# Scores of a query block in two neighbouring banks, and narrow exponentials shared by heads, in an attention and expert-layer kernel

## The chip, the core and the metric

The kernel runs on one core of one Trainium2 chip. The metric is the device time of one execution in microseconds, as the median of several executions. A core has a matrix engine (TensorE, PE in the profile; PEld is its weight load), a vector engine (VectorE, DVE), a scalar engine (ScalarE, ACT), GpSimd (POOL) and SyncE (SP), which issues DMAs. Each takes its instructions in order. Matrix products are written to PSUM, which has 8 banks of 512 float32 columns on 128 partitions; ACT and DVE read them from there.

## The reference

The input x has 4 batches of 1024 tokens with 256 features. The first layer is causal attention with 16 heads of 16 features, whose queries, keys and values go through a latent of 64; half of each head's features are turned by rotary embeddings. The second layer has 8 experts, of which each token takes 2, chosen by a router with three Sinkhorn rounds.

```python
q = concat([q_c, rope(q_e)]); k = concat([k_c, rope(k_e)])
att = softmax(where(causal, q @ k.T / sqrt(16), -inf))
x = layernorm(x + (att @ v) @ Wc)
gates = sinkhorn((x @ router_w.T + router_b) / temperature, 3)
w, idx = top_k(gates, 2)
out = sum(w_j * ((relu(x @ wg[idx_j]) * (x @ wp[idx_j])) @ wo[idx_j]))
x = layernorm(x + (x + out))
```

## The kernel before

The program is written as one stream of instructions, and the framework orders each engine's queue by priority (program order, which some parts move forward) and by a planned time line; it also gives out the buffers of each pool and adds the waits. So a tile of a pool can be taken when an earlier one of that pool has been read for the last time.

**PSUM.** Eight banks, in four pools: `ps_mx` (3 banks), `ps_st` (2), `ps_bg` (2) and `ps_ac` (1, sums of attention times values). `any_tile` hands out banks of the first three in turn, for the start and the end, where no attention needs them.

**Attention** goes over units: a batch and a group of 4 heads, with queries in two halves of 512 (in the last batch the halves are units of their own). It makes the scores twice.

- `row_max` (L342) makes them as queries by keys, 128 queries at a time, in `mx` tiles of one bank (L354, L355). For the first half of the queries there is one score tile of 128 to 512 keys, for the second half a full one of 512 and then one of 128 to 512. A full tile off the diagonal is reduced by `tensor_reduce` (L361), one on the diagonal by an instruction that adds the causal mask and takes the maximum (L364). L370 merges the two maxima. The 16 columns of maxima of 4 heads and 4 query blocks are then transposed (L373, in an `mx` bank), negated and split into two bfloat16 rows by ACT and DVE (L375, L376), and two small DMAs from the ACT queue put them under the queries as rows 96 and 97.
- `attend` (L399) makes them as keys by queries, a key block of 128 at a time, for 4 heads in turn, in `st` tiles of one bank (L433, L434); the two extra rows subtract the maxima. ACT takes the exponential into `pT` (L438), one instruction for each head. On the four diagonal key blocks of a half the columns shrink: 512, 384, 256, 128. POOL sets what lies above the diagonal to zero (L447; in the last two units DVE does, L443). `values` (L412) multiplies by the values (L418) and ACT copies the sum out (L423).

**Side work** is given out in small steps beside attention, and all of it takes its PSUM tiles from `ps_bg`: `project` (queries and keys of a coming batch in four chunks of 128 rows, then values), `finish` (normalize y, output projection, layer norm, logits of the router), and `route` (Sinkhorn, top 2, positions in lists that are scattered to memory by POOL's indirect DMAs). The row maxima get a priority 200 ahead, and may run 44 steps ahead of attention (`LEAD`). The first expert is gathered while the last batch's attention runs. The finish of the last half runs alone, with banks from `any_tile` and `own_tile`.

**Experts** follow: `slot` (L963 on) takes 512 rows of one expert, or 256 for the further ones, makes gate and linear part in `mx` tiles in four chunks, ACT and DVE evacuate them (L977, L978), and the output goes through `st` tiles and is added to memory by indirect DMAs. A last layer norm reads the rows back.

Of the kernel before, what the change touches and what calls it, by code (L numbers as in the profile page):

```python
# [9 lines left out]
F32 = mybir.dt.float32  # L10
# [6 lines left out]
N_MX, N_ST, N_BG = (3,2,2)  # L17
# [10 lines left out]
NMX = 1  # L28
# [7 lines left out]
P = 128  # L36
# [7 lines left out]
def kernel(  # L44
# [60 lines left out]
    def mx_tile(name):  # L105
        return ps_mx.tile([P, QC], F32, tag="mx", name=name)
# [7 lines left out]
    turn = [0]  # L114

    def any_tile(name):

        turn[0] += 1
        return (mx_tile, bg_tile, mx_tile, st_tile, bg_tile, mx_tile, st_tile)[turn[0] % 7](name)
# [30 lines left out]
    for half in range(NQC):  # L150
# [8 lines left out]
    mask = const.tile([P, QC], F32, name="mask")  # L159
    nc.gpsimd.memset(mask, 0.0)  # L160
    nc.gpsimd.affine_select(
        out=mask[:, QC - P :], in_=mask[:, QC - P :], pattern=[[-1, P]], compare_op=ALU.is_ge,
# [72 lines left out]
    def project(b, half, tile_):  # L235
# [40 lines left out]
        pair = []  # L276
        for o in range(2):
            pair.append(chunk(o))
            yield 1.3
        for o in range(2):  # L280
            t1 = proj.tile([P, QC], F32, tag="t1", name=f"t1_{n}_{o}", bufs=R_BUFS)
            nc.vector.tensor_tensor(t1, pair[o], rope[:, 2 * o, cols], ALU.mult)
            t2 = proj.tile([P, QC], F32, tag="t2", name=f"t2_{n}_{o}", bufs=R_BUFS)
            nc.vector.tensor_tensor(t2, pair[1 - o], rope[:, 2 * o + 1, cols], ALU.mult)
            lean.tensor_tensor(t1, t1, t2, ALU.add)
            store(o, t1, lean, [(qk, DHE + o * DHE // 2, DHE // 2) for qk in range(2)])
            yield 0.2
# [54 lines left out]
    def row_max(unit):  # L342

        b, gs, qcs = unit
        for g, half in [(g, qc) for g in gs for qc in qcs]:
            q, k = stack(unit, g)
            n = f"{b}_{g}_{half}"
            mx = work.tile([P, NQC, HG * BPQ], F32, tag="mx", name=f"mx{n}", bufs=2)
            for h in range(HG):
                for t in range(BPQ):  # L350
                    t0 = half * QC + t * P
                    for k0 in range(0, t0 + P, QC):
                        w = min(t0 + P - k0, QC)
                        ps = mx_tile(f"s{n}_{h}_{t}_{k0}")  # L354
                        nc.tensor.matmul(  # L355
                            ps[:, :w], lhsT=q(h, half)[:NROW, t * P : (t + 1) * P], rhs=k(h, k0 // QC)[:NROW, :w],
                            start=True, stop=True,
                        )
                        m = mx[:, k0 // QC, h * BPQ + t : h * BPQ + t + 1]
                        if k0 < half * QC:  # L360
                            nc.vector.tensor_reduce(m, ps, AX.X, ALU.max)  # L361
                        else:
                            dump = work.tile([P, QC], BF16, tag="dump", name=f"d{n}_{h}_{t}", bufs=2)
                            nc.vector.tensor_tensor_reduce(  # L364
                                out=dump[:, :w], in0=ps[:, :w], in1=mask[:, QC - w :],
                                scale=1.0, scalar=MASKED, op0=ALU.add, op1=ALU.max, accum_out=m,
                            )
                        yield
            for j in range(1, half + 1):
                nc.vector.tensor_tensor(mx[:, 0], mx[:, 0], mx[:, j], ALU.max)  # L370
            R = HG * BPQ
            tp = mx_tile(f"mxT{n}")
            nc.tensor.transpose(tp[:R, :P], mx[:, 0], ident)  # L373
# [25 lines left out]
    def attend(unit):  # L399
# [25 lines left out]
        for g, qc in [(g, qc) for g in gs for qc in qcs]:  # L425
            q, k = stack(unit, g)
            for kb in range((qc + 1) * BPQ):
                lo = max(0, kb * P - qc * QC)
                n = f"{b}_{g}_{qc}_{kb}"
                pT = exps.tile([P, HG, QC], F32, tag="pT", name=f"pT{n}")  # L430
                for h in range(HG):
                    late = unit in units[len(units) - NMX :]
                    st = (mx_tile if late and h % 2 else st_tile)(f"sT{n}_{h}")  # L433
                    nc.tensor.matmul(  # L434
                        st[:, lo:], lhsT=k(h, kb // BPQ)[: NROW + 2, kb % BPQ * P : (kb % BPQ + 1) * P],
                        rhs=q(h, qc)[: NROW + 2, lo:], start=True, stop=True,
                    )
                    nc.scalar.activation(pT[:, h, lo:], st[:, lo:], AF.Exp, scale=scale)  # L438
# [875 lines left out]
```

## Time and profile before

| | |
|---|---|
| median of 9 runs | 1121.56 us (1112.28 to 1129.08) |
| profiled execution | 1117.93 us; span of its instructions 1116.2 us |
| mean granted TensorE clock | 0.953 |
| first score matmul of `row_max` / of `attend` | 48.6 us / 67.7 us |
| last score matmul of `attend` | 740.7 us |
| experts' first / last gate matmul | 744.6 us / 1074.9 us |

A profile line of a group reads: line, engine, operation, output and inputs by the program's names, shapes, count, then busy time in all and mean nanoseconds of one, then the engine's idle time just before these and what ended it. A wait line reads: who waited, for whom, total, times and the longest. A timeline line reads: start, length, engine, what, how many in a row, and the idle time before. Matmuls overlap and their ends are modelled, so a busy TensorE need not be at its peak.

### The profile page before, as it was taken

The page shows a single profiled execution, that of the slowest core. Times are in us where ns is not written, and L with a number is a line of the kernel's source. Part 1 is how long each engine was busy: PE and PEld are TensorE (multiplying, and loading weights), DVE is VectorE, ACT ScalarE, POOL GpSimd, SP SyncE. Part 2 cuts the span into 40 slices and gives each one's busy share as a digit, 9 for nine tenths or more (in the row PEclk, how much of TensorE's full clock was granted, in tenths as well). Part 3 has the DMA queues.
Part 4 walks back from the last instruction along what each step waited for, and adds up shares of the span by engine and source line. Part 5 has one row for each costly group of instructions (what it writes and reads, how often), then busy time and mean ns, then how long its engine had stood idle before and what let it go on. Part 6 is the DMA issues. An engine that isn't in the chain of part 4 may idle for free.

```text
span 1116.2 us, 18329 instructions
## 1 busy us (share of the span) xinstructions
PE 987.1 (88%) x6040; PEld 580.7 (52%) x6040; DVE 751.8 (67%) x2300; ACT 643.4 (58%) x1474; POOL 481.8 (43%) x551
## 2 busy tenths in 40 slices
PE   6688999999999998999799799599999799999960
PEld 4444333355434254533244233158888688888860
DVE  4778777888987786887437688147667345646536
ACT  3445666656766564676566576366555355656633
POOL 7167511121635422441423402632566786554544
PEclk9889999999999998999999999699999899999995
DMA  7573420231331330441123220136655356665647
GB/s 261 165 212 111 115 66 15 77 115 40 100 105 29 92 97 19 136 112 49 49 70 114 61 61 3 27 123 188 157 110 147 90 103 161 125 164 101 160 60 301
DMA packets 71367, 119.68 MB, mean 107 GB/s; under 512 B 16416, under 2 KB 43040, under 8 KB 70880
## 3 DMA queue, kind: packets, MB, share of 16 engines
q1 hardware_dynamic: 48544, 81.76, 23.7%
q0 software_dynamic: 20672, 36.41, 15.1%
q8 instruction: 50, 0.82, 0.3%
q10 hardware_dynamic: 2048, 0.27, 0.2%
q14 instruction: 53, 0.43, 0.1%
HBM read 82.52 MB, written 35.60 MB: 106 GB/s over the span
## 4 chain that ended last, share of the span: by engine, by line
PE 72%; ACT 8%; DVE 7%; DMA 5%; issue 5%; SPq 2%; another core or an unknown queue 1%; POOL 1%; ACTq 0%; DVEq 0%; POOLq 0%
PE y L418 14%; PE sT L434 11%; PE s L355 10%; ACT pT L438 4%; PE gp L197 3%; PE gp L198 3%; PE gp L196 3%; PE po L594 3%; PE eo L196 3%; PE eo L198 3%; PE eo L197 3%; PE lp L197 2%; PE lp L198 2%; PE lp L196 2%; DVE mx L361 2%
## 5 line engine op out<-in xcount | busy, mean ns | idle before, releaser
L438 ACT ACTIVATE pT<-sT 128x512 f32<-128x512 f32 (+3 forms) x768 | 347.8, 491 | 210.2 <-PE sT L434 155.9
L364 DVE CUSTOM_DVE_ANT_0 d<-s,mask 128x128 bf16<-128x128 f32 (+3 forms) x512 | 238.0, 483 | 68.1 <-PE s L355 51.7
L434 PE MATMUL sT<-qs,ks 98*128 98x512 bf16 (+3 forms) x768 | 235.2, 334 | 32.8 <-ACT pT L438 16.3
L355 PE MATMUL s<-ks,qs 96*128 96x512 bf16 (+3 forms) x768 | 224.5, 334 | 27.9 <-DMA ks<-parts 7.7
L447 POOL TENSOR_SCALAR_AFFINE_SELECT pT<-pT 128x512 f32<-128x512 f32 x120 | 76.7, 640 | 285.6 <-ACT pT L438 269.3
L361 DVE TENSOR_REDUCE mx<-s 128x1 f32<-128x512 f32 x256 | 175.3, 685 | 31.0 <-PE s L355 28.8
L418 PE MATMUL y<-pT,va 128*32 128x512 f32 (+3 forms) x1536 | 186.1, 512 | 1.1 <-POOL pT L447 0.9
L355 PEld LDWEIGHTS <-qs 96*128 96x128 bf16 x768 | 72.0, 99 | 138.5 <-issue 106.8
L434 PEld LDWEIGHTS <-ks 98*128 98x128 bf16 x768 | 72.5, 99 | 128.7 <-issue 98.0
L995 POOL DMA_INDIRECT results<-eo,ents x64 | 104.8, 1638 | 79.3 <-ACT eo L994 63.3
L196 PE MATMUL eo<-wh,hh 128*128 128x256 f32 x280 | 81.3, 292 | 6.5 <-ACT eo L994 6.4
L190 DVE TENSOR_TENSOR wl<-w,wh 128x512 fp32r<-128x512 f32 x108 | 69.9, 684 | 21.3 <-ACT wh L189 19.9
L921 POOL DMA_INDIRECT xg<-x_rows,ents x64 | 65.3, 1021 | 41.6 <-PE xgT_ps L960 19.7
L978 DVE TENSOR_TENSOR relu<-relu,lp 128x512 f32<-128x512 f32 x64 | 43.8, 684 | 57.2 <-ACT relu L977 23.1
L418 PEld LDWEIGHTS y<-pT,va 128*32 128x32 f32 x1536 | 33.4, 109 | 88.9 <-issue 54.7
L197 PE MATMUL eo<-wl,hh 128*128 128x256 f32 x280 | 79.5, 285 | 0.0
L813 POOL DMA_INDIRECT pairs<-ent,so_i x64 | 65.9, 1030 | 29.5 <-issue 18.1
L198 PE MATMUL eo<-wh,hl 128*128 128x256 f32 x280 | 77.9, 284 | 0.0
L977 ACT ACTIVATE relu<-gp 128x512 f32<-128x512 f32 (+1 forms) x76 | 42.7, 563 | 60.9 <-PE gp L198 40.9
L190 DVE TENSOR_TENSOR hl<-relu,hh 128x512 fp32r<-128x512 f32 (+1 forms) x76 | 48.6, 647 | 28.1 <-ACT hh L189 20.8
L189 ACT CAST wh<-w 128x512 fp32r<-128x512 f32 x108 | 60.5, 619 | 9.5 <-PE gp L197 6.3
L196 PE MATMUL gp<-xh,wh 128*128 128x512 f32 (+1 forms) x176 | 63.6, 368 | 2.2 <-issue 1.1
(209 smaller groups left out, 1795.0 us busy)
## 6 DMA issues: line engine op xcount, KB each, us to landing
ks<-parts SPq DMA_DIRECT2D x90, 128.0 KB
w<-in_wg_dram SPq DMA_DIRECT2D x18, 512.0 KB
w<-in_wp_dram SPq DMA_DIRECT2D x18, 512.0 KB
w<-in_wo_dram SPq DMA_DIRECT2D x18, 512.0 KB
qs<-parts SPq DMA_DIRECT2D x66, 128.0 KB
parts<-lv POOLq DMA_DIRECT2D x12, 384.0 KB
parts<-lv POOLq DMA_DIRECT2D x24, 192.0 KB
xh<-in_x_t_dram SPq DMA_DIRECT2D x8, 512.0 KB
```

The lines of the kernel that those rows point to most:

```text
L190: (sub or nc.vector).tensor_tensor(lo, src, hi.bitcast(F32), ALU.subtract)
L196: nc.tensor.matmul(ps, lhsT=sh, rhs=mh, start=(i == 0), stop=False)
L197: nc.tensor.matmul(ps, lhsT=sh, rhs=ml, start=False, stop=False)
L198: nc.tensor.matmul(ps, lhsT=sl, rhs=mh, start=False, stop=(i == n - 1))
L355: nc.tensor.matmul(ps[:, :w], lhsT=q(h, half)[:NROW, t * P : (t + 1) * P], rhs=k(h, k0 // QC)[:NROW, :w], start=True, stop=True,)
L361: nc.vector.tensor_reduce(m, ps, AX.X, ALU.max)
L364: nc.vector.tensor_tensor_reduce(out=dump[:, :w], in0=ps[:, :w], in1=mask[:, QC - w :], scale=1.0, scalar=MASKED, op0=ALU.add, op1=ALU.max ...
L418: nc.tensor.matmul(acc[g, qc][SLOT * h : SLOT * (h + 1), lo:], lhsT=va[b % 2][:, kb, at : at + SLOT], rhs=pT[:, h, lo:], start=(kb == 0), ...
L434: nc.tensor.matmul(st[:, lo:], lhsT=k(h, kb // BPQ)[: NROW + 2, kb % BPQ * P : (kb % BPQ + 1) * P], rhs=q(h, qc)[: NROW + 2, lo:], start=T ...
L438: nc.scalar.activation(pT[:, h, lo:], st[:, lo:], AF.Exp, scale=scale)
L447: diagonal[0] = nc.gpsimd.affine_select(out=block, in_=block, pattern=[[0, HG], [1, P]], compare_op=ALU.is_ge, fill=0.0, base=0, channel_m ...
L995: ins = nc.gpsimd.indirect_dma_start(out=results[:, :], out_offset=bass.IndirectOffsetOnAxis(ap=k.ent[:, j, 1:2], axis=0), in_=eo, in_offs ...
```

## The change

- An `mx` tile is two neighbouring banks, and there are 2 of them; `bg` has one bank. `st` and `ac` stay at 2 and 1.
- In `row_max`, both score tiles of a query block of the second half lie in one `mx` tile, and one masked instruction over 640 to 1024 columns takes their maximum; L361 and L370 are gone. In the first half, two query blocks share an `mx` tile, a bank each, with an instruction each as before. The mask is bfloat16 and 1024 wide. The transpose of the maxima goes to a `bg` tile.
- In `attend`, two heads share an `st` bank where the columns are 256 and four where they are 128, with one exponential for all of them. In the last unit, where the columns are 384 or 512, the first two heads take a bank each of an `mx` tile and share an exponential.
- In `project`, each of the two chunks with rotary features is multiplied by both tables at once, right behind its matmuls; there are four buffers for the products where there were two.
- In `finish`, the logits take a tile for each two token blocks, which is added to the bias at once, where one tile held four.
- `any_tile` and `own_tile` hand out halves of `mx` tiles; `rows` of the first expert and the last `finish` use `st` tiles; gate and linear part of an expert chunk lie in one `mx` tile.
- `prepare` zeroes rows of the results from a tile of its own, not from the mask.

```diff
-N_MX, N_ST, N_BG = (3,2,2)
+N_MX, N_ST, N_BG = (2,2,1)
     def mx_tile(name):
-        return ps_mx.tile([P, QC], F32, tag="mx", name=name)
+        return ps_mx.tile([P, 2 * QC], F32, tag="mx", name=name)
...
-        return (mx_tile, bg_tile, mx_tile, st_tile, bg_tile, mx_tile, st_tile)[turn[0] % 7](name)
+        if not (turn[0] % 7) % 2:
+            if not spare:
+                both = mx_tile(name)
+                spare.append(both[:, QC:])
+                return both[:, :QC]
+            return spare.pop()
+        return (bg_tile, st_tile, st_tile)[turn[0] % 7 // 2](name)
...
-        pair = []
+        own, others = [], []
         for o in range(2):
-            pair.append(chunk(o))
+            ps = chunk(o)
+            for of, tag, row in ((own, "own", 2 * o), (others, "oth", 3 - 2 * o)):
+                t = proj.tile([P, QC], F32, tag=f"{tag}{o}", name=f"{tag}{n}_{o}", bufs=R_BUFS)
+                nc.vector.tensor_tensor(t, ps, rope[:, row, cols], ALU.mult)
+                of.append(t)
             yield 1.3
         for o in range(2):
...
-            lean.tensor_tensor(t1, t1, t2, ALU.add)
+            lean.tensor_tensor(own[o], own[o], others[1 - o], ALU.add)
...
                 for t in range(BPQ):
-                    t0 = half * QC + t * P
-                    for k0 in range(0, t0 + P, QC):
-                        w = min(t0 + P - k0, QC)
-                        ps = mx_tile(f"s{n}_{h}_{t}_{k0}")
+                    if half or t % 2 == 0:
+                        both = mx_tile(f"s{n}_{h}_{t}")
+                    at = 0 if half else t % 2 * QC
+                    w = half * QC + (t + 1) * P
+                    for k0 in range(0, w, QC):
+                        m = min(w - k0, QC)
                         nc.tensor.matmul(
...
-                        if k0 < half * QC:
-                            nc.vector.tensor_reduce(m, ps, AX.X, ALU.max)
-                        else:
+                        if k0 + m == w:
...
+                                out=dump[:, :w], in0=both[:, at : at + w], in1=mask[:, T - w :], scale=1.0,
+                                scalar=MASKED, op0=ALU.add, op1=ALU.max,
+                                accum_out=mx[:, h * BPQ + t : h * BPQ + t + 1],
...
-            for j in range(1, half + 1):
-                nc.vector.tensor_tensor(mx[:, 0], mx[:, 0], mx[:, j], ALU.max)
-            tp = mx_tile(f"mxT{n}")
+            tp = bg_tile(f"mxT{n}")
...
+                late = unit in units[len(units) - NMX :]
+                w = QC - lo
+                m = QC // w if w < 3 * P else 1
                 for h in range(HG):
-                    late = unit in units[len(units) - NMX :]
-                    st = (mx_tile if late and h % 2 else st_tile)(f"sT{n}_{h}")
+                    two = late and m == 1 and h < 2
+                    if two and h == 0:
+                        both = mx_tile(f"sT{n}_{h}")
+                    if two:
+                        st = both[:, h * QC :]
+                    elif h % m == 0:
+                        st = st_tile(f"sT{n}_{h}")
...
-                    nc.scalar.activation(pT[:, h, lo:], st[:, lo:], AF.Exp, scale=scale)
+                    if two and h:
+                        nc.scalar.activation(
+                            pT[:, :2, lo:], both.rearrange("p (h t) -> p h t", t=QC)[:, :, :w], AF.Exp, scale=scale
+                        )
+                    elif not two and h % m == m - 1:
+                        nc.scalar.activation(
+                            pT[:, h + 1 - m : h + 1, lo:], st[:, : m * w].rearrange("p (h t) -> p h t", t=w),
+                            AF.Exp, scale=scale,
+                        )
...
+        none = exps.tile([P, HG * QC], F32, tag="pT", name="none")[:, :C]
+        nc.vector.memset(none, 0.0)
...
-                if alone and turn[0] % 3 == 0:
+                if not alone or turn[0] % 3 == 1:
+                    return bg_tile(name)
+                if turn[0] % 3 == 0:
                     return ps_ac.tile([P, QC], F32, tag="ac", name=name)
-                return bg_tile(name)
+                return mx_tile(name)[:, :QC]
...
-                if not rts:
-                    rts[0] = own_tile(f"rt{n}")
+                if i % 2 == 0:
+                    rts[i // 2] = own_tile(f"rt{n}_{i}")
...
-            if 2 * R > QC:
-                gate, lin = (mx_tile(f"{i}p{k.name}_{f}") for i in "gl")
-            else:
-                both = mx_tile(f"gp{k.name}_{f}")
-                gate, lin = both[:, :R], both[:, R:]
+            both = mx_tile(f"gp{k.name}_{f}")
+            gate, lin = both[:, :R], both[:, R : 2 * R]
...
-    rows(first[0], bg_tile)
+    rows(first[0], st_tile)
```

## The prediction

> **What bounds the kernel now.** I read the page first, then stretches of time, groups by form, waits of TensorE and the timeline of single queues. On the page (busy time by engine, then busy tenths in 40 slices of 27.9 us):
>
> ```profile
> PE 987.1 (88%) x6040; PEld 580.7 (52%) x6040; DVE 751.8 (67%) x2300; ACT 643.4 (58%) x1474; POOL 481.8 (43%) x551
> PE   6688999999999998999799799599999799999960
> DVE  4778777888987786887437688147667345646536
> ACT  3445666656766564676566576366555355656633
> ```
>
> TensorE looks full, VectorE follows it up to slice 25 (attention) and not behind that (experts). Stretches say it closer: a piece of attention without side work, then a piece of the experts (columns: length, then PE, PEld, DVE, ACT, POOL, granted clock, DMA share, GB/s).
>
> ```profile
> 120.00:212.00 92.00, 85.65 (x539) 28.52 (x538) 73.25 (x251) 58.74 (x141) 17.16 (x28) 1.00 0.26 77
> 960.00:1000.00 40.00, 39.77 (x237) 34.87 (x236) 20.69 (x33) 21.86 (x43) 24.01 (x20) 1.00 0.64 159
> ```
>
> In the experts TensorE has 0.23 us of 40 free: nothing the change does there can bring more than that. In attention TensorE is at 93%, VectorE at 80%, ScalarE at 64%, and the 93% is flattering: a lone 512-wide score matmul lasts 0.38 us, but two in a row take 0.60 together, so they can start every 0.22 us, and what lies between is latency that counts as busy. The groups by form give the prices:
>
> ```profile
> L438 ACT ACTIVATE pT<-sT 128x512 f32<-128x512 f32 x384 | 215.5, 599 | 106.9 <-PE sT L434 79.7 <-PE s L355 5.3 <-remote 4.7
> L438 ACT ACTIVATE pT<-sT 128x256 f32<-128x256 f32 x128 | 45.6, 383 | 33.9 <-PE sT L434 28.0 <-PE s L355 2.5 <-DVE tk_m L739 0.9
> L438 ACT ACTIVATE pT<-sT 128x128 f32<-128x128 f32 x128 | 31.6, 276 | 35.1 <-PE sT L434 21.8 <-remote 6.0 <-PE y L418 2.2
> L361 DVE TENSOR_REDUCE mx<-s 128x1 f32<-128x512 f32 x256 | 175.3, 685 | 31.0 <-PE s L355 28.8 <-remote 1.1
> L364 DVE CUSTOM_DVE_ANT_0 d<-s,mask 128x512 bf16<-128x512 f32 x128 | 87.3, 682 | 11.8 <-PE s L355 11.6
> L364 DVE CUSTOM_DVE_ANT_0 d<-s,mask 128x128 bf16<-128x128 f32 x128 | 36.2, 283 | 25.4 <-PE s L355 20.3 <-PE sT L434 2.6 <-remote 2.2
> ```
>
> ScalarE and VectorE wait for TensorE there, and TensorE for them (waits of TensorE: total, times, longest):
>
> ```profile
> PE sT L434 <- ACT pT L438: 16.3, 38, 6.0
> PE s L355 <- DVE mx L364: 7.4, 21, 0.9
> PE s L355 <- DVE mx L361: 2.1, 8, 0.4
> PE x1T_ps L584 <- ACT x1T L587: 0.7, 2, 0.4
> PE v_ps L196 <- DVE t L284: 0.6, 1, 0.6
> ```
>
> So attention is bound by rings of few banks between three engines, none of them full. ScalarE's timeline of one diagonal shows where the exponentials cost most:
>
> ```profile
> 130.57 0.92 ACT L438 ACTIVATE pT<-sT 128x384 f32<-128x384 f32 x2 [1.03 <-PE y L418]
> 132.38 1.13 ACT L438 ACTIVATE pT<-sT 128x256 f32<-128x256 f32 x3 [0.89 <-PE s L355]
> 134.27 0.38 ACT L438 ACTIVATE pT<-sT 128x256 f32<-128x256 f32 x1 [0.76 <-PE sT L434]
> 135.48 1.03 ACT L438 ACTIVATE pT<-sT 128x128 f32<-128x128 f32 x4 [0.82 <-PE s L355]
> 137.43 1.09 ACT L438 ACTIVATE pT<-sT 128x512 f32<-128x512 f32 x2 [0.92 <-PE sT L434]
> ```
>
> Four heads 256 wide hold their place 3.10 us (132.38 to 135.48), four 128 wide 1.95 us.
>
> **The change, part by part.** Unit below means one head group of one batch, 16 in all, each with 8 diagonal key blocks; without side work one takes 35.0 us (126.95 to 161.97 between its copies of y).
>
> *Narrow exponentials.* At 256 columns two heads share a bank, at 128 four; at 384 and 512 nothing changes. 128 instructions of 383 ns become 64 of 512 columns (599), 128 of 276 become 32 of 599: 49.0 - 38.3 = 10.7 us, and 35.3 - 19.2 = 16.2 us, 26.9 us of ScalarE in 160 fewer instructions (0.168 us each, which is also the fixed part of a line through 276 and 599). The timeline is more careful: the four 128-wide ones took 1.03 in a row, one takes 0.60, so 0.43 for each of 32 blocks, 14 us; they stood alone between two TensorE waits, so I count them whole. The 256-wide ones take three in 1.13, four in 1.51 without their wait, against some 1.14 for two: 0.37 x 32 = 12 us; but VectorE ran in that stretch without a gap and TensorE carried value matmuls, so I count half, 6. Value -20 us; ends 0 (all of it hidden behind the reductions) and -35 (the handshakes before them, 33.9 + 35.1 us of idle, shrink too). Set against that, the Trainium skill (ScalarE: Activation LUTs, "What ACT_TABLE_LOAD costs") gives an ACTIVATE with immediate scale and bias 186 ns + 0.833 ns a column, with 93 ns of overlap back to back. By it a removed one is worth 93 ns where they queue: 160 x 0.093 = 15 us in place of 27.
>
> *Row maxima.* For the second half of the queries, a 685 ns reduction and a masked one become a single masked one over 640 to 1024 columns. By the line through 283 (128) and 682 (512), 1.04 ns a column, the 512 more columns cost 532 in place of 685: 0.153 x 256 = 39 us, and the 16 merges at L370 (4.3 us by their group) go: 43 us. Added: eight more 0.19 us additions of logits (1.5) and a memset. In the first half the count stays. VectorE is at 80% and TensorE's shown wait for it is 9.5 us, so I count a quarter, -10; ends 0 and -42.
> Its price is the ring. Three single banks become two pairs, and a pair is given back after one instruction of 0.15 + 1.04 x 640..1024 = 0.82 to 1.21 us, not 0.69. With the other pair full, VectorE still has about 1 us in hand, which is a burst of value matmuls (1.06 us for eight). The Trainium skill (PSUM — Partial Sum Buffer, "PSUM bank collisions raise a hardware error") says two engines must not meet in one bank, which speaks against this: a reduction over a pair can start only behind both matmuls. No run here shows a collision; by the rule alone each of 256 pairs starts 0.22 us later, 56 us if nothing covered it. From the rows: shown waits are 9.5/29 = 0.33 us each; one in 20 pairs more gives +4, my value; ends 0 and 0.13 x 256 = +34 (the longer release).
>
> *One bank for the side work.* Projection of batches 1 to 3 (6 halves x 6 tiles), finish of seven halves (12 tiles each, the logits' tile now twice), routing of three batches (4 each) and all 32 transposes of maxima (which leave the mx ring) share it: 36 + 84 + 12 + 32 = 164 tiles. The rope products now leave the bank at once (0.69 x 2 us), where before a pair of chunks stayed until both halves were multiplied: same 32 products, cost nothing on VectorE. TensorE's queue is in order, so a side matmul that waits for the bank holds the scores behind it. Before, such waits were rare, 0.3 to 0.7 us when they came. Lower end: as rare as in the full score rings, 25.8 us in 1536 tiles, 0.017 x 164 = 3 us. Upper end: every tile waits 0.35: 57 us. I take 0.05, nearer the rings, because the order is planned for one bank: +8.
> Long tenants are a case of their own. The routing tile sk_tp is held from 280.2 to 290.4 in its first turn, and a yt tile fills as head groups end:
>
> ```profile
> 614.06 0.44 PE L568 MATMUL yt_ps<-ident,yT 128*128 128x128 f32 x2
> ...
> 614.61 0.27 PE L373 MATMUL mxT<-ident,mx 128*16 128x128 f32 x1
> ...
> 629.35 0.38 PE L568 MATMUL yt_ps<-ident,yT 128*128 128x128 f32 x2
> ```
>
> With one bank the transpose at 614.61 waits until the yt tile is read, some 15 us. Row maxima run ahead (the unit it serves starts about 628), so most is covered; behind it queue its ACT and DVE copies, two small DMAs and then all scores of that unit. In the last batch the finish, routing and gather also lead to the first expert (740 us). Value +4, ends 0 and +25.
>
> *Small edits, one answer.* Two pT buffers instead of one are held by DMAs in prepare: +2 (0 to 5; POOL's queue gets no new DMA). Experts: gate and linear part in one pair, four banks for three; the 256-row slots have two tiles for three: 0, ±3, covered by 39.77 of 40. The last finish takes halves of mx tiles: 0 to +6, since it leads to the gather at 880 (840 to 920 has 8 us of TensorE idle). Start: the front is bound by DMA waits of about 6 us: 0, ±3. In the last unit, six pair exponentials: -1, left in rounding.
>
> Sum: -20 - 10 + 4 + 8 + 4 + 2 = -12. The profiled execution took 1117.93 (span 1116.2 and 1.7 around it), 3.6 under the median of nine, 1121.56. 1117.9 - 12 + 3.6 = 1109.5, say **1110**.
>
> **The rivals.** *The single bank decides (slower).* Place: the head of TensorE's queue, between 210 and 510 us where finish, projection and routing overlap. At 0.35 us a tile it takes 57 and the rest gives 12 + 8 = 20 back: +37, 1158; it turns the sign at 20/164 = 0.12 us a tile. For: sk_tp and yt hold banks over 10 us, and both banks were often in use at once. Against: gaps such as 120 to 212 have no side work at all, so the total fits. Chance 0.27; with a fair mean of 0.22 us, 36 - 20 = +16, 1137.
> *The pair ring decides (slower).* The +34 end with the other terms of the sum: -12 - 4 + 34 = +18, about 1140. For: VectorE is the fullest engine after TensorE. Against: four banks for three. Chance 0.12.
> *Nothing moves.* Exponentials and reductions turn into time at half of what I count, and the costs stand: -10 - 5 + 4 + 8 + 4 + 2 = +3, 1124. This is also the case in which the change doesn't do what it says: 384-wide heads are not shared, and in the first half no reduction goes. Chance 0.14.
> Forecast, 1085 to 1115: 0.47.
>
> **How the numbers follow.** A measurement here can tell about 0.5% from no change, 5.6 us. Faster 0.47, same 0.14, slower 0.27 + 0.12 = 0.39. The range leaves a tenth at each side: below, -35 - 10 + 8 = -37, 1085; above, the single bank at about 0.3 us a tile, 49 - 20 = +29, 1150. The forecast's own range is 1085 to 1115.
>
> **What would show it.** Right: 64 + 32 exponentials of 512 columns more and none of 128 or 256 wide alone; ScalarE near 616, VectorE near 710; the units of 120 to 212 shorter by 1.5 to 2; TensorE busy less by a few us only. Wrong: waits of qk_ps, ynT_ps, po, mxT or sk_tp on TensorE adding to over 15 us (the bank), or s waiting for mx by over 25 us (the ring). If ScalarE and VectorE fall as counted and the unit stays at 35 us, the conversion into time failed.

## The result, and the profile after

The change makes the kernel slower: 1236.63 us (median of 20 runs, 1229.07 to 1245.01) against 1120.62 us (62 runs, 1112.28 to 1131.11), ratio 1.1049 [1.1029, 1.1069]. The forecast was 1110, the range ended at 1150.

The page of the changed kernel, busy time by engine and then four of its rows of 40 slices (31 us each):

```profile
PE 1034.8 (83%) x6040; PEld 601.3 (48%) x6040; DVE 763.5 (62%) x2037; ACT 631.0 (51%) x1308; POOL 479.2 (39%) x551
PE   6569899998789989699898785987995999999970
DVE  4666677686588567488558876325673454564545
ACT  3335666752365655166664152573562554565543
PEclk9879899998689999699998796887998899999995
```

ACT falls to 2, 1, 1 and 2 in slices 10, 17, 23 and 25 (its lowest digit before was 3), and the granted clock to 6 in slices 11, 17 and 25. Stretches show these holes (columns as before); the first row is the stretch of attention that the prediction showed, the last one is a piece of the experts:

```profile
120.00:212.00 92.00, 82.75 (x537) 33.38 (x535) 65.91 (x171) 57.81 (x114) 31.16 (x42) 0.96 0.32 96
280.00:320.00 40.00, 30.49 (x155) 16.77 (x154) 21.71 (x72) 9.17 (x22) 7.06 (x10) 0.78 0.25 81
480.00:520.00 40.00, 30.87 (x192) 17.07 (x188) 21.28 (x72) 12.75 (x28) 8.72 (x13) 0.80 0.33 103
720.00:760.00 40.00, 26.44 (x149) 13.19 (x148) 28.09 (x106) 13.77 (x38) 5.08 (x7) 0.74 0.15 44
1020.00:1060.00 40.00, 39.91 (x234) 34.37 (x233) 22.79 (x37) 23.00 (x45) 23.26 (x19) 1.00 0.54 116
```

In the holes ScalarE works 9 to 14 us of 40, where it worked 58.74 of 92 in attention before (25.5 of 40). The experts run as full as they did. The groups by form say that each instruction costs what the prediction had taken from its lines:

```profile
L457 ACT ACTIVATE pT<-sT 128x512 f32<-128x512 f32 x470 | 264.2, 598 | 125.8 <-PE sT L447 91.3 <-PE y L423 8.1 <-PE s L364 4.9
L457 ACT ACTIVATE pT<-sT 128x384 f32<-128x384 f32 x126 | 58.9, 496 | 30.8 <-PE sT L447 28.6 <-DVE mx L370 0.8 <-PE sk_tp L715 0.7
L370 DVE CUSTOM_DVE_ANT_0 d<-s,mask 128x1024 bf16<-128x1024 f32 x64 | 78.1, 1220 | 15.9 <-PE s L364 10.0 <-PE sT L447 3.0
L370 DVE CUSTOM_DVE_ANT_0 d<-s,mask 128x640 bf16<-128x640 f32 x64 | 52.6, 822 | 15.6 <-PE s L364 8.0 <-PE po L620 3.0 <-PE mxT L378 1.0
```

A maximum over 1024 columns takes 1.22 us and one over 640 takes 0.82, as the line said. The waits of TensorE, on the other hand, are new:

```profile
PE s L364 <- DVE mx L370: 39.5, 73, 4.2
PE xgT_ps L989 <- ACT eo L1020: 15.2, 1, 15.2
PE sT L447 <- ACT pT L457: 10.4, 34, 0.9
```

The scores wait 39.5 us for the pair ring, 30.0 more than before. That is still not the loss. Time goes in two places (the profiled executions lie 124 us apart, the medians 116): the last copy of y comes at 835.6 us, not 743.5 (92 us), and what lies behind it takes 404.5 us, not 372.8 (32 us). Between the copies of y that end a unit lie 41, 36, 40, 39, **82**, 45, 38, 42, **76**, 33, 35 us, and the unit over the hole at 720 us takes **118**. These three units are 138 us longer than their counterparts (42.2, 41.2 and 54.9 us); the others give 44 of that back.

The timeline of TensorE in the first hole, behind the last reduction of one head group's maxima on VectorE (first fence; its last line is the first of the next group):

```profile
286.98 1.23 DVE L370 CUSTOM_DVE_ANT_0 d<-s,mask 128x1024 bf16<-128x1024 f32 x1 [0.22 <-PE s L364]
288.13 0.08 DVE L370 DVE_READ_ACCUMULATOR2_ANT mx<- 128x1 f32 x1
288.36 0.29 DVE L370 CUSTOM_DVE_ANT_0 d<-s,mask 128x128 bf16<-128x128 f32 x1
```

```profile
303.37 0.63 PE L594 MATMUL yt_ps<-ident,yT 128*128 128x128 f32 x4 [0.45 <-DVE yn L601]
...
305.45 0.48 PE L364 MATMUL s<-ks,qs 96*128 96x512 bf16 x2
305.87 0.44 PE L610 MATMUL ynT_ps<-ident,yn 128*128 128x128 f32 x2
307.11 1.13 PE L620 MATMUL po<-wc_sb,ynT 128*128 128x256 f32 x4 [0.80 <-ACT ynT L613]
308.75 1.13 PE L620 MATMUL po<-wc_sb,ynT 128*128 128x256 f32 x4 [0.52 <-DVE x L623]
312.97 0.69 PE L610 MATMUL x1T_ps<-ident,x 128*128 128x128 f32 x2 [3.09 <-DVE x L548]
...
319.94 1.88 PE L630 MATMUL rt<-rwT,x1T 128*128 128x8 f32 x8 [0.52 <-ACT x1T L613]
...
324.39 0.63 PE L204 MATMUL qk_ps<-xT_h,wqk_l 128*128 128x512 f32 x1
326.42 0.38 PE L378 MATMUL mxT<-ident,mx 128*16 128x128 f32 x1 [1.40 <-DVE r L268]
```

The maxima are complete at 288.2 us. Their transpose, 0.38 us of work, runs at 326.42. In between the one side bank goes from a yt tile to ynT, po, x1T, rt and a qk chunk, and each tenant waits for ACT or DVE before the next may enter. From 305.9 to 327.7 no score matmul runs at all, ScalarE's last exponential ended at 288.1 and the next comes at 332.6, and in the holes the granted clock falls to 0.74 to 0.80. Scores for the exponentials (sT) stand still from 287 to 332 us here, and in the same way from 493 to 531, from 676 to 710 and from 732 to 759 us.

The maxima are also hardly ahead. A half is here one head group with 512 of a batch's queries; two halves make a unit. In the six halves before this hole, 3 to 12 us lie between the last maximum of a half and its first score for the exponentials; in the kernel before it is 10 to 44 us in the same six, and 30 us (261.2 to 291.0) in the half over the hole. So here a late transpose is felt at once.

### The profile page after: what moved, and what is told of

Same layout as the page of the kernel before. It is cut to its first block, busy times and chain, and to the rows that moved or that the text cites. A ratio compares the mean times of both kernels' runs of the same rounds, so it can differ in the third digit from the quotient of the medians.

```text
span 1240.0 us, 17871 instructions
## 1 busy us (share of the span) xinstructions
PE 1034.8 (83%) x6040; PEld 601.3 (48%) x6040; DVE 763.5 (62%) x2037; ACT 631.0 (51%) x1308; POOL 479.2 (39%) x551
## 4 chain that ended last, share of the span: by engine, by line
PE 64%; DVE 14%; ACT 7%; issue 6%; DMA 4%; SPq 2%; another core or an unknown queue 1%; POOL 1%; ACTq 0%; DVEq 0%; POOLq 0%
PE y L423 11%; PE s L364 9%; PE sT L447 8%; DVE d L370 6%; PE gp L202 5%; PE gp L203 5%; PE gp L204 5%; ACT pT L457 4%; PE po L620 3%; PE eo L202 2%; PE eo L204 2%; PE eo L203 2%; DVE wl L196 2%; SPq L343 2%; PE qk_ps L202 2%
## 5 line engine op out<-in xcount | busy, mean ns | idle before, releaser
L370 DVE CUSTOM_DVE_ANT_0 d<-s,mask 128x128 bf16<-128x128 f32 (+7 forms) x512 | 386.0, 754 | 147.0 <-PE s L364 112.8
L457 ACT ACTIVATE pT<-sT 128x512 f32<-128x512 f32 (+1 forms) x596 | 320.4, 576 | 156.6 <-PE sT L447 119.9
L364 PE MATMUL s<-ks,qs 96*128 96x512 bf16 (+3 forms) x768 | 219.3, 352 | 47.0 <-DVE mx L370 39.5
L447 PE MATMUL sT<-qs,ks 98*128 98x512 bf16 (+3 forms) x768 | 216.6, 343 | 25.4 <-ACT pT L457 10.4
L423 PE MATMUL y<-pT,va 128*32 128x512 f32 (+3 forms) x1536 | 173.2, 524 | 0.5 <-POOL pT L469 0.4
L202 PE MATMUL gp<-xh,wh 128*128 128x512 f32 (+1 forms) x304 | 117.0, 391 | 5.8 <-ACT xh L195 2.6
L203 PE MATMUL gp<-xl,wh 128*128 128x512 f32 (+1 forms) x304 | 116.3, 383 | 0.0
L204 PE MATMUL gp<-xh,wl 128*128 128x512 f32 (+1 forms) x304 | 115.1, 379 | 0.0
L1004 DVE TENSOR_TENSOR relu<-relu,gp 128x512 f32<-128x512 f32 (+1 forms) x76 | 48.9, 643 | 92.4 <-ACT relu L1003 66.2
L842 POOL DMA_INDIRECT pairs<-ent,so_i x64 | 63.3, 990 | 41.7 <-DVE nm L381 23.1
```

Source lines behind the costliest of these rows:

```text
L202: nc.tensor.matmul(ps, lhsT=sh, rhs=mh, start=(i == 0), stop=False)
L203: nc.tensor.matmul(ps, lhsT=sh, rhs=ml, start=False, stop=False)
L204: nc.tensor.matmul(ps, lhsT=sl, rhs=mh, start=False, stop=(i == n - 1))
L364: nc.tensor.matmul(both[:, at + k0 : at + k0 + m], lhsT=q(h, half)[:NROW, t * P : (t + 1) * P], rhs=k(h, k0 // QC)[:NROW, :m], start=True, ...
L370: nc.vector.tensor_tensor_reduce(out=dump[:, :w], in0=both[:, at : at + w], in1=mask[:, T - w :], scale=1.0, scalar=MASKED, op0=ALU.add, o ...
L423: nc.tensor.matmul(acc[g, qc][SLOT * h : SLOT * (h + 1), lo:], lhsT=va[b % 2][:, kb, at : at + SLOT], rhs=pT[:, h, lo:], start=(kb == 0), ...
```

## The experiments

Two kinds of chip were met: on some the kernel before takes 1073 to 1074 us, on others 1120 to 1126. Each ratio is against runs of the kernel before on the same chip; its time is given. The changed kernel itself was measured beside a before of 1121.

**The kernel before again, and the exponentials alone.** e0 is the kernel before, unchanged.

> The kernel before, unchanged, for a profile on the chip of the runs beside it. Every theory: the time of before, ratio 1.00 within 0.5%.

Measured (before 1122.04): 0.9986 [0.9954, 1.0018].

e2 is the kernel before with the shared exponentials and nothing else:

```diff
+                    if h % m == 0:
                         st = st_tile(...)
-                    nc.scalar.activation(pT[:, h, lo:], st[:, lo:], AF.Exp, scale=scale)
+                    if h % m == m - 1:
+                        nc.scalar.activation(pT[:, h + 1 - m : h + 1, lo:], st[:, : m * w]..., AF.Exp, scale=scale)
```

> The kernel before with only the shared narrow exponentials (two heads at 256 columns, four at 128), all banks as before. By the term of the prediction, 20 us faster: 1095 to 1110. If the reductions of VectorE hide it: 1115 to 1126. If an exponential that waits for four matmuls costs more than it saves: above 1130.

Measured (before 1074.27): 0.9955 [0.9923, 0.9986], some 5 us, not the 20 of the prediction. e6 takes them out of the changed kernel (`m = 1`; the shared pair of the last unit stays):

> The changed kernel with an exponential for each head again (in the last unit the first two heads still share). Against e4_one_bank_mxT (ratio 1.075), which has three single mx banks and separate reductions in place of two pairs, it tells what pairs and merged reductions do. Theory A: 1.075 to 1.09, the ring costs little, the shared exponentials nothing. Theory B: 1.10 to 1.13, the pairs cost 3 to 5%.

Measured (before 1122.04): 1.1049 [1.0984, 1.1114], the same as with them and in theory B's range. ScalarE's busy time is 647.4 us against 631.0, so the instructions did get cheaper by 16.4 us; nothing waited for that.

**Where the transposes of the maxima lie.** e1 puts them back into an `mx` tile, in the changed kernel, e10 into an `st` tile:

```diff
-            tp = bg_tile(f"mxT{n}")
+            tp = mx_tile(f"mxT{n}")    # e1
+            tp = st_tile(f"mxT{n}")    # e10
```

> The changed kernel with one line undone: the transpose of the row maxima takes an mx tile again, not the single bg bank. Theory A (the transposes of the maxima queue behind the side work's tiles in the one bank, and attention stands still until they come: 304 to 330, 503 to 530 and 680 to 760 us of the changed kernel): 70 to 110 us go, 1125 to 1165 us. Theory B (the ring of two pairs is too short for VectorE and TensorE): nothing changes but noise, 1225 to 1245. Theory C (the single bank slows finish, projection and routing themselves, and these set the end): 10 to 30 us go, 1205 to 1225.

Measured (before 1074.27): 1.0933 [1.0887, 1.0979]. The three long units are gone, as in theory A, but the others are longer, some 43 us each, and the time is near theory B's: a transpose now keeps one of only two pairs, and TensorE's transposes wait 16.7 us for the maxima.

> The changed kernel with the transposes of the maxima in the exponentials' banks (st), so neither in the side bank nor in the pair ring. If the pair ring's own price is the 3.0% of e6 against e4 and one bank costs 2.6%: about 1.056, no unit over 55 us. If the pairs cost more, and the side bank's stalls only hid it: 1.08 or more, with units of 40 to 44 us all through.

Measured (before 1119.71): 1.0368 [1.0318, 1.0417], less than either case had. The last copy of y comes at 744.4 us, as in the kernel before (743.5), although the second comes at 135.2 and not at 127.0, and the stretch that was a hole is full:

```profile
280.00:320.00 40.00, 39.09 (x262) 19.11 (x261) 32.17 (x100) 25.75 (x56) 7.90 (x12) 1.00 0.20 61
```

So one line of the change, the transposes' bank, makes 6.8 of the 10.5 points, and the attention with pairs, one side bank and shared exponentials is neither faster nor slower than before. The pairs cost less than I had read from e6 against e4 (3 points).

The same line in the kernel before, with one side bank (e3 without it, e4 with it; the side edits of the change come along, since one bank needs them), and with two (e8, e9):

> The kernel before with one bg bank in place of two (one bank of PSUM unused), with the edits of the side work that one bank needs (rope products at once, logits in two tiles, other banks for the last finish); maxima, their transposes and exponentials as before. Theory A: 1120 to 1145, since the transposes have their own ring. Theory C: above 1180, most of the loss of the change.

> As e3_one_bank, but the transposes of the row maxima go to the bg bank as in the changed kernel. Theory A: 60 to 110 us slower than e3_one_bank, 1190 to 1240, with stalls of attention of 20 us and more behind finish. Theories B and C: within 10 us of e3_one_bank.

Measured (before 1074.27): e3 1.0261 [1.022, 1.0303], e4 1.0748 [1.071, 1.0786], with units of 71, 73 and 83 us. By the ratios both lie just outside theory A's ranges (e3 up to 1.022, e4 at least 5.4 points above e3), and far from those of B and C.

> The kernel before with the side edits of the one-bank version (each rope product leaves its chunk at once, logits of a finish in two tiles added by halves, the last finish also in score tiles) but still two side banks. Theory A (the 2.6% of the one-bank version is the missing bank): 1.00 +- 0.005. Theory B (the edits themselves cost): 1.01 to 1.026.

> The kernel e8 with the transposes of the maxima in the side banks, of which there are two. Theory A (the transposes stand behind a chain of finish tiles, in whatever number of banks the side work has): 1.03 to 1.06, units of over 55 us as with one bank. Theory B (the wait comes of there being one bank: with a second, the transpose has the other): within 0.01 of e8 and no unit over 50 us.

Measured (before 1119.71): e8 1.0043 [1.0013, 1.0073], e9 1.0341 [1.0275, 1.0407]. A second bank takes the first two long units away (50 us at most) and leaves the last, 90.5 us, where the routing of the third batch holds the banks. TensorE's timeline of e9:

```profile
671.81 0.38 PE L691 MATMUL sk_tp<-ident,sk_pm 128*8 128x128 f32 x1 [0.60 <-DVE sk_pm L688]
672.72 0.38 PE L700 MATMUL sk_tp<-ident,sk_es 128*8 128x128 f32 x1 [0.53 <-DVE sk_es L698]
674.66 0.59 PE L723 MATMUL sk_tp<-sk_dg,ones 8*128 8x8 f32 x2 [1.57 <-DVE sk_dg L721]
680.11 0.23 PE L789 MATMUL so_ps<-so_m,before 128*128 128x64 bf16 x1 [4.85 <-DVE so_m L782]
680.16 0.40 PE L373 MATMUL mxT<-ident,mx 128*16 128x128 f32 x1
```

The transpose comes right behind the last waiting tenant. So it is the chain of tenants that makes it late; a second bank takes the price from 4.7 points (1.0748/1.0261) to 3.0 (1.0341/1.0043).

What a late transpose costs depends on how far the maxima are ahead. In e4 the three transposes come 54, 57 and 43 us behind their maxima, and the scores for the exponentials stand still for 26, 28 and 29 us. In e9 they come 36, 34 and 34 us behind them, and the scores stand 0, 2 and 25 us: in the last batch the maxima are less ahead (12 to 14 us in e8). In the changed kernel the first two come 38 and 39 us behind, hardly more than in e9, and the scores stand 45 and 39 us.

**Why the transpose can't pass.** e5 gives the transposes and their copies the highest priority in the changed kernel (`with tc.high_priority(offset=4000):` around them).

> The changed kernel, with the transposes of the maxima and what follows them (two copies, two DMAs) ranked ahead of the side work when the queues are ordered; banks as in the change. Theory A (the loss is that they rank behind finish's tiles in the one bank): the stalls of 20 us and more go, ratio to before 1.02 to 1.05 where the change has 1.105. Theory B (the ring of two pairs paces the maxima, and attention waits for these): 1.08 to 1.105, units evenly longer instead of three stalls.

Measured (before 1122.04): 1.1033 [1.097, 1.1096], and the transpose runs at 325.6 us. That is theory B's time but not its picture: three long units stay (82, 75 and 117 us). e11 leaves the priorities and changes the order in which the program asks:

```diff
         if g == 1 and 0 < b < B - 1 or g == 0 and last and qcs[0] == 1:
+            while (step := next(maxima, None)):
+                maxed += step
             lane.until(f"F{b - 1}")
```

> The changed kernel; ahead of each forced run of a finish (lane.until of F0, F1, F2) the maxima of the head group under way are asked for to their end: 4 more score steps (20 at F2), so that their transpose stands in front of the finish's tiles in the order in which the program asks for the bank. Theory A (the bank is handed out in the order of the requests): the stalls at 304, 503 and 680 us go, no unit over 60 us, 1.06 to 1.085. Theory B (the bank goes by rank or by readiness, or the finish itself holds the attention): 1.10, the stalls of 75 us and more stay.

Measured (before 1119.71): 1.1122 [1.1074, 1.117]. The time is nearer to theory B, the trace is what theory A had. The transpose that was asked for before the finish now passes it; the next one, asked for behind it, comes when it came before (345.62 in the changed kernel):

```profile
300.67 0.28 PE L378 MATMUL mxT<-ident,mx 128*16 128x128 f32 x1
...
345.71 0.38 PE L378 MATMUL mxT<-ident,mx 128*16 128x128 f32 x1 [1.38 <-DVE oth L287]
```

The two units over it take 48.5 and 72.2 us instead of 81.9 and 44.5. The stall has moved by one head group and is 6 us shorter. So the bank is handed out in the order of the requests, whatever the priority; I had been wrong to expect that a stall moved is a stall gone. e12 gives the maxima and their negatives four buffers, so that later reductions can go on:

```diff
-            mx = work.tile([P, HG * BPQ], F32, tag="mx", name=f"mx{n}", bufs=2)
+            mx = work.tile([P, HG * BPQ], F32, tag="mx", name=f"mx{n}", bufs=4)
```

> The changed kernel with four buffers for the maxima and for their negatives instead of two, so that the reductions of later head groups can go on while a transpose waits. Theory A (the attention stops because the maxima run out of buffers): 1.05 to 1.08, units under 60 us. Theory B (the attention itself waits for the late transpose, and reductions done meanwhile give back only what they would have cost later): 1.08 to 1.105, units of 60 us and more stay, since the transpose still stands behind the finish in the bank's order.

Measured (before 1072.59): 1.0965 [1.0918, 1.1012], with units of 85, 81 and 97 us: theory B. The attention itself waits for the late transpose. (How the changed kernel stands on this kind of chip wasn't measured, so what the buffers bring is not known to the point.)

**A fourth score bank.** e7 is e3 with four single `mx` banks for three, as many as two pairs have.

> e3_one_bank (ratio 1.026) with the unused bank given to the mx ring: four single banks in place of three, separate reductions, transposes in the mx ring. Theory B (what counts is how many score tiles VectorE has in hand): 1.00 to 1.02. If the single bank of the side work is all that costs in e3_one_bank: 1.02 to 1.03.

Measured (before 1122.04): 1.0345 [1.0285, 1.0404]. In the total it doesn't help, but its attention isn't slower: the last copy of y comes at 732.1 us, in e8, with two side banks on the same kind of chip, at 735.6. Behind it e7 takes 418.2 us and e8 381.4.

**Behind the attention.** All of e10's loss lies there: 406.4 us behind the last copy of y, 372.8 before. In the kernel before the first gate tile of the experts comes 1 us behind that copy, in e10 19 us. e17 gives the kernel before the change's tiles for the last finish, and nothing else:

```diff
-                if alone and turn[0] % 3 == 0:
-                    return ps_ac.tile(...)
-                return bg_tile(name)
+                if not alone or turn[0] % 3 == 1:
+                    return bg_tile(name)
+                if turn[0] % 3 == 0:
+                    return ps_ac.tile(...)
+                return mx_tile(name)
...
-    rows(first[0], bg_tile)
+    rows(first[0], st_tile)
```

> The kernel before with one side edit alone: the last finish takes side, accumulator and score tiles in turn, its transposes of y the exponentials' tiles, and the first slot's rows too. Theory A (the experts' first gate tiles stand behind the last finish in the order of the score tiles): first gate tile 15 to 25 us after the last copy of y, instead of 1; behind that the experts go faster, since TensorE has the finish out of the way, and 1.005 to 1.01 stays. Theory B (the early gate tiles come of something else, as the logits in two tiles): first gate tile within 5 us, 1.00 +- 0.003.

Measured (before 1125.76): 1.0154 [1.0108, 1.02]. The gate tiles are late as in theory A, by 21 us, but more is lost than it had, since the experts don't go faster for it (331.7 us from the first to the last gate tile, 330.3 before). The gate tiles use `mx` tiles too and now stand behind the finish's:

```profile
765.03 1.87 PE L586 MATMUL x1T_ps<-ident,x 128*128 128x128 f32 x6 [3.15 <-issue]
766.70 0.86 PE L605 MATMUL rt<-rwT,x1T 128*128 128x8 f32 x4
767.41 0.77 PE L196 MATMUL gp<-xh,wh 128*128 128x512 f32 x1
```

The last copy of y was at 746.3. e8 had the same late gate tile and lost less (rest 381.4 us), so how much of the delay is made good later differs.

The other piece is a gap of 15.2 us in the experts (the wait of xgT_ps above), which stands at 857 us in e10 too. POOL's queue there:

```profile
844.36 1.00 POOL L842 DMA_INDIRECT pairs<-ent,so_i  x1 [0.30 <-DVE table L886]
...
864.18 0.97 POOL L842 DMA_INDIRECT pairs<-ent,so_i  x1 [0.30 <-issue]
865.45 1.60 POOL L1021 DMA_INDIRECT results<-eo,ents  x1 [0.30 <-issue]
```

Sixteen scatters of the last batch's pairs take 21 us, and the experts' outputs queue behind them until their six buffers are full. e14 is e10 with ten such buffers (`EO = 10`) and with the first unit's transposes in the side bank; e15 is e2 with ten buffers; e13 is e10 with one exponential a head.

> The kernel e10 with the first unit's two transposes in the side bank (in e10 the first copy of y comes at 103 us, not 87 to 89) and ten buffers of expert outputs instead of six (in e10 TensorE stands 15.2 us at 857 us). If both are what they seem: 10 to 15 us earlier at the start and 10 to 15 us in the experts, 1.010 to 1.020, and no gap of TensorE over 8 us in the experts. If the gap is a wait for something else (the gather, weights): the gap stays, about 1.025. That it beats the kernel before: not expected.

> The kernel before with the shared exponentials alone (0.9955) and ten buffers of expert outputs instead of six. The gap of TensorE in the experts is 5.9 us in the kernel before. If the buffers end it: 0.988 to 0.993, the fastest of all. If the gap is a wait for something else: 0.9955 +- 0.003.

> The kernel e10 (changed, transposes in st) with one exponential for each head. Theory A (the shared exponentials are worth time once nothing stops the attention, as my -20 us had it): 1.050 to 1.056 against e10's 1.037. Theory B (they are worth what they were in the kernel before, 0.45%): 1.038 to 1.046. Theory C (nothing, as in the changed kernel): 1.034 to 1.038.

Measured (before 1072.59): e14 1.0424 [1.0391, 1.0457], e15 0.9924 [0.9899, 0.9948], e13 1.0465 [1.0419, 1.0511]. e14's gap is gone, but so it is in e1, e12 and e13, which have six buffers and ran on the same kind of chip. So e14, slower than both its cases, doesn't show what the buffers do, and its start gained nothing (second copy of y at 141.4 us, in e10 at 135.2). e13 lies 0.4 points over e14, with intervals that overlap: the shared exponentials may be worth as much here as alone. e15 lies in the range for the buffers, but its interval overlaps that of e2, and e2's trace, with six buffers, has no gap over 3 us there either. e16 adds to e15 the rope products that leave their chunk at once:

> The kernel e15 (before, shared exponentials, ten buffers of expert outputs: 0.9924) with rope products that leave each projected chunk at once. In e8, which had this among its edits, the attention ended 4 to 8 us sooner than in the kernel before. If that is the rope's doing: 0.985 to 0.989. If not: 0.9924 +- 0.003.

Measured (before 1125.76): 0.9946 [0.9911, 0.998]: no further gain. Its trace has a wait of 7.1 us in the same place of the experts with ten buffers, so buffers alone don't end it. What sets the length of that gap stays open.

The fastest version that was run is e15, before with shared exponentials and ten output buffers, 0.8% faster than the kernel before; by the ratios, which come from both kinds of chip, the changed one takes 11% longer than it.

## Why the prediction was wrong

The forecast failed in one step; besides, two costs were too small, and the saving of the row maxima is not in the traces.

**The step that failed** is "Long tenants are a case of their own", which gave the transposes in the single bank +4 us, ends 0 and +25. They cost 76 us (1236.6 - 1120.6 = 116; e10 lost 40). I had found the right place: the transpose behind a yt tile, 15 us, and all scores of the next unit behind it. Two things were wrong. I priced one tenant, where the wait is for every tile asked for earlier, and `lane.until("F0")` asks for a whole finish at a stroke, a chain of tenants that each wait for another engine. And I wrote "Row maxima run ahead ..., so most is covered". In the changed kernel they run 3 to 12 us ahead before the first hole, where they were 10 to 44 ahead in the kernel before: at 288.2 us the maxima of this half are complete, the exponentials of the half before it have just ended (288.1), and the wait of 38 us until 326.4 is covered by nothing. In e9, where they are ahead, the scores stand still for 0 and 2 us over waits of 36 and 34.

**One bank for the side work**, +8, ends 3 and 57: e3 against e8 says 2.2 points, some 24 us, if chips of both kinds may be compared, and e7 against e8, on one kind, 3.0 (e7 has a fourth score bank besides). But a price for each of the tiles in the attention is not what the traces show: e7's attention ends 3.5 us before e8's, and e10's when that of the kernel before does. The loss lies behind it, where this term had none: with one side bank the first gate tile comes 28.4 (e3) and 29.6 us (e7) behind the last copy of y, with two 18.8 (e8), and e7 has a gap of 12.6 us in the experts.

**Small edits**: the last finish was put at 0 to +6 and costs 17 us by e17 (e8, which has it among other edits, lost only 5 in all, and I can't say what gave the rest back). I saw that it "leads to the gather", and missed that the experts' gate tiles take the same pool and so lose their place at the front. "Experts ... 0, ±3" held for the pace (39.91 of 40), not for the gap on POOL.

**Narrow exponentials**, -20, ends 0 and -35: the mechanism holds, the conversion does not. The durations of all exponentials in the trace fell from 377.0 to 349.5 us, by 27.5 where 26.9 had been counted, and ScalarE's busy time, in which an overlap counts once, by 16.4 (e6 to the changed kernel). Of that 5 us arrive alone and none in the changed kernel. The Trainium skill (ScalarE: Activation LUTs, "What ACT_TABLE_LOAD costs") gives an ACTIVATE with immediate scale and bias a fixed part of 186 ns, of which 93 ns overlap with the next one back to back; 160 fewer would make 15 us by that, as an estimate. The 16.4 us measured here (158 fewer) agree with it, and not with the 0.168 us each that I had from the line.

**Row maxima**, -10: added up by the groups, their instructions fell from 422.7 to 386.0 us, 4 more with the merges, nearly as worked out. But these durations overlap, and from start to start the maxima got slower. In the kernel before:

```profile
179.96 0.69 DVE L361 TENSOR_REDUCE mx<-s 128x1 f32<-128x512 f32 x1
180.56 0.68 DVE L364 CUSTOM_DVE_ANT_0 d<-s,mask 128x512 bf16<-128x512 f32 x1
181.17 0.08 DVE L364 DVE_READ_ACCUMULATOR2_ANT mx<- 128x1 f32 x1
181.17 0.69 DVE L361 TENSOR_REDUCE mx<-s 128x1 f32<-128x512 f32 x1
```

Here 1024 columns take 1.21 us, where the durations add up to 1.45; in the changed kernel they take 1.38 (286.98 to 288.36 in the timeline of the first hole). Where the next maximum follows directly, the medians for 768, 896 and 1024 columns are 1.11, 1.24 and 1.38 us, for 0.95, 1.08 and 1.21 before. So a pair costs 0.16 us more, where I had 0.153 less; over 256 pairs this is up to some 40 us of VectorE, an estimate from these rows. VectorE's busy time did not fall either: it is 754.3 us in e10, where the attention doesn't stand still, and 754.7 in e8, which has the old maxima.

What makes the difference is the time behind a maximum. In the kernel before, a masked maximum that follows another starts within 0.02 us of the accumulator's read (`DVE_READ_ACCUMULATOR2_ANT`) in 132 of 168 cases, in the changed kernel in none of 292: it starts 0.12 us behind the read of one over 256 or 512 columns and mostly 0.23 us behind the read of a wider one, and most of these waits are put down to the maximum before it. The change has something that its list leaves out: the masked output, which nothing reads, has one buffer where it had two. That fits, but no run changed it alone. Without the 0.23 us a pair would take some 0.06 us less than before, 16 us in all, as an estimate.

**Pair ring**, +4, ends 0 and +34: TensorE's wait for it grew by 30.0 us, yet e10, with 30.7 us of such waits, ends the attention when the kernel before does. (Its end of +34 counted the longer release of the narrowest pair alone, 0.82 us for 0.69; the widest takes 1.22.) So all terms of the attention but the transposes came to about nothing together, where I had -18; they were not told apart further. What ring and slower maxima take away is part of the lead: in e10 it is 8 to 20 us in the six halves where the kernel before has 10 to 44. Which of the two takes how much, and why the changed kernel has only 3 to 12 there, was not separated.

So of the rivals "the single bank decides" had the right resource, and "For: sk_tp and yt hold banks over 10 us" the right sign, but it was priced by the tile (1158) and not by the chain. Of the signs named beforehand, ScalarE "near 616" (631.0) and VectorE "near 710" (763.5) both failed, the units of 120 to 212 us got longer instead of shorter (40.9 and 35.9 us for 35.0 and 35.4), and the ring's wait of over 25 us was met without deciding anything. The sign for the bank was right: the waits of qk_ps, ynT_ps, po, mxT and sk_tp add up to some 40 us, over the 15 named. But mxT itself has 10 of them; the 38 us of one late transpose are put to the tenants before it, a few tenths to 3 us each. A queue of tenants shows as late starts in the timeline, hardly as a line in the list of waits.

What is left open: of e10's 34 us behind the attention, 9 are the longer gap (15.2 for 5.9) and about 18 the late start; some 7 are not assigned. What the change would do with a second buffer for the masked output was not run.

## What to carry to other kernels

Before a small step that others wait for is moved into a pool with one buffer, list every tile that the program asks for before it, add up their waits on other engines, and compare that with the lead the step has, in the kernel as it will be and not as it was; the busy share of the bank says nothing on that. A priority moves instructions in a queue, not requests in a pool: give such a step a buffer of its own, or one of a ring whose tenants leave fast (here `st`, 6.8 points). Fewer and wider instructions can shorten an engine's work, but not the time, where the engine waits for another one anyway. And take the price of an instruction from start to start in a timeline: the fixed part that a duration shows may lie under its neighbours already.

## What the runs showed of the hardware that was not expected

- The same kernel takes 1073 to 1074 us on some chips and 1120 to 1126 on others, with instruction times that agree (a 512-wide exponential 598 to 601 ns, a 512-wide maximum 683 to 685 ns in traces from both). The granted clock of these executions of the kernel before was 0.967 to 0.976 on the first and 0.943 to 0.956 on the others. Effects of a few per cent had to be compared on one chip.
- TensorE's granted clock follows the holes: 0.74 to 0.80 where the attention stands still, 1.00 in the first two of these stretches when it doesn't (e10, 280 to 320 and 480 to 520 us). In the first hole a projection chunk's matmuls of 512 columns follow each other by 0.43 us at a granted clock of 0.50 (322 to 325 us), where those of the experts follow by 0.23 at a clock of 1.00.
- VectorE's maxima overlap at their ends: for 1024 columns, durations of 1.45 us take 1.21 from start to start in the kernel before. In the changed kernel, with one buffer for the masked output, a maximum over 1024 columns lasts 1.22 us and the next starts 1.38 behind its start.
